# A fused two-layer kernel on one core: Pi's rows spread over a head's channels by DMA through DRAM in place of TensorE, and the products with Pi a tile later

## The chip, the cores and the metric

The kernel runs on one core of a Trainium2 chip, in one launch, in fp32 throughout. The metric is the device time in microseconds (us), the median over several executions. Engines are named as in the profile: PE is TensorE (PEld its weight loads), DVE is VectorE, ACT is ScalarE, POOL is GpSimd, SP is the engine that issues most DMA transfers.

## What is computed

Two layers over x of shape (2, 768, 64, 64): a state-space block (layer 0), then an attention without a score matrix (layer 1). Each layer takes a group norm of its input and adds its result to it. The change lies in layer 1, for which the reference is, with HEADS = 12, d = 64 channels per head and N = 4096 positions:

```python
w = (x3 @ W_qkv.T).reshape(B, N, HEADS, d).transpose(0, 2, 1, 3)
norm = jnp.sqrt(jnp.sum(w * w, axis=2, keepdims=True))
w_normed = w / jnp.maximum(norm, 1e-12)
logits = jnp.sum(w_normed ** 2, axis=-1) * temp
Pi = jax.nn.softmax(logits, axis=1)                      # over the 12 heads
Pi_n = Pi / (jnp.sum(Pi, axis=-1, keepdims=True) + 1e-08)
dots = jnp.einsum('bhn,bhnd->bhd', Pi_n, w ** 2)[:, :, None, :]
attn = 1.0 / (1.0 + dots)
out = -(w * Pi[..., None]) * attn                        # then @ W_out.T
```

So Pi has one value per head and position, and each is used for all 64 channels of its head.

## The kernel before

**Layout.** Channels lie on the 128 partitions, in KM = 6 chunks of 128 (two heads each), and positions along the free axis, in NQ = 8 tiles of QL = 512 positions per image. A matrix product of one chunk of outputs by one tile takes six 128x512 matmuls over the six input chunks; each fp32 matmul shows as two records in the trace.

**Order of the work.** Everything is issued in program order, written out by hand, each engine in its own in-order queue. Layer 0 runs to about 2780 us. Then, for image 0, the qkv products run in a block form with fewer multiplications (`strassen`), then `attention(0, ...)`, then a second `strassen` run (W_out for image 0, qkv for image 1), then `attention(1, ...)`, then W_out for image 1. Twelve ordinary products are kept back for each attention stage, so that TensorE has work while the softmax goes through the other engines. In the stage of image 0 they are qkv products of image 1, evicted by ScalarE (`p1_evict`, lines 677 and 678); in that of image 1 they are W_out products of image 0, evicted by VectorE with the residual addition (`p3_evict`, line 707) and stored. `half_a` issues three of a product's six matmuls (and the loads for the product three ahead), `half_b` the other three, then what it is handed, then the eviction.

**One tile of attention**, in the order of the steps:

- `squares`: ScalarE squares the six chunks of w (line 984), two tiles ahead.
- `head_rows`: TensorE sums the squares per head with weights `gcol` into `pr` (line 1006); ScalarE copies it to `lt` (line 1009).
- `head_columns`: four matmuls turn the 12 head rows into columns, `pl` (line 1017), positions on the partitions.
- `softmax_a`: VectorE takes the maximum `mx` (line 1023) and subtracts it (line 1025), ScalarE takes the exponential (line 1026).
- `softmax_b`: VectorE sums, takes the reciprocal and multiplies (lines 1032 to 1034), writes the result four times side by side into `pi` with padding (line 1036) and adds up `ph` (line 1037); TensorE transposes `pi` into `pt` (line 1041), ScalarE copies it to `pit` (line 1045).
- `spread`: for each chunk one matmul with the 0/1 weights `esel` repeats the two head rows of `pit` over 64 partitions each, into PSUM tiles `ppz` and `ppo` (line 1057).
- `times_pi`: VectorE multiplies w by the spread Pi (line 1063).
- `pi_sums`: VectorE multiplies that by w again and sums it up into `dots` (line 1070, with an accumulator read after it).

The loop over tiles j in `attention` overlaps the row and column steps and the softmax of tile j + 1 with the spread, products and sums of tile j. After the loop come one product, the sum of Pi over all positions `pp` (line 1107), `at` = -1/(1 + dots) on VectorE (lines 1112 to 1119), `behind()`, which issues the first loads of the next `strassen` run and scales its first tile by `at` (line 824), and one more product.

Of the kernel before, what the change touches and what calls it, by code (L numbers as in the profile page):

```python
# [7 lines left out]
F32 = mybir.dt.float32  # L8
# [6 lines left out]
P = 128  # L15
# [51 lines left out]
@with_exitstack  # L67
def both_layers(
    ctx, tc, nc, consts, x, in_wP, xp_wP, dt_wP, out_wT, pc_in, comb_in, pick_in, xsum_in, gavg_in, gsel_in, wo_dr, bc_dr, s_dr, x1, stats1,
    qkvP, woutP, temp_c, hcol_in, hsel_in, esel_in, out  # L70
):
    ident, ones, eps_c = consts

# [552 lines left out]
    ss = [gp.tile([P, KM, 2 * NQ], F32, name=f"ss{b}") for b in range(NB)]  # L626
    for t in ss:
        nc.gpsimd.memset(t, 0.0)
    x1s, w1s, pis, pits, ats, dots, phs = {}, {}, {}, {}, {}, {}, {}

    def gn_next(b):
        mv = gp.tile([P, KM, 2], F32, name=f"mv1_{b}")
# [126 lines left out]
    def product(n=1):  # L759
        for _ in range(n):  # L760
            half_a()
            half_b()
# [238 lines left out]
    def head_rows(b, j):  # L1001
        pr = psX.tile([P, 512], F32, tag="px", name=f"pr{b}_{j}")
        for m in range(KM):
            w2 = sqs.pop((b, j, m))
            r = 32 * (m % 4)
            nc.tensor.matmul(pr[r : r + 32, :], gcol[:, m, :], w2, start=(m < 4), stop=(m in (2, 3, 4, 5)))  # L1006
            give(w2)
        lt = wk.tile([P, QL], F32, tag="du", name=f"lt{b}_{j}", bufs=2)
        nc.scalar.copy(lt, pr)
        pits["lt"] = lt  # L1010

# [17 lines left out]
    def softmax_b(b, j):  # L1029
        e = pis.pop("e")  # L1030
        sm = small.tile([P, NB4], F32, tag="sm", name=f"sm{b}_{j}")
        nc.vector.tensor_reduce(sm, e, AX.X, ALU.add)
        nc.vector.reciprocal(sm, sm)
        nc.vector.tensor_mul(e, e, sm.unsqueeze(2).to_broadcast([P, NB4, HEADS]))
        pi = pi4[j % 2]
        nc.vector.tensor_copy(pi[:, :, :, :HEADS], e.unsqueeze(2).to_broadcast([P, NB4, 4, HEADS]))
        nc.vector.tensor_reduce(phs[b][:, j, :], e.rearrange("p q h -> p h q"), AX.X, ALU.add)

        pt = psS.tile([P, 512], F32, tag="st", name=f"pt{b}_{j}")
        for q in range(NB4):  # L1040
            nc.tensor.matmul(  # L1041
                pt[:, q * P : (q + 1) * P], pi[:, q, :, :].rearrange("p c h -> p (c h)"), ident, start=True, stop=True
            )
        pit = wk.tile([P, QL], F32, tag="delta", name=f"pit{b}_{j}", bufs=3)
        nc.scalar.copy(pit, pt)
        pits[b, j] = pit

    def spread(b, j, ms):

        for m in ms:  # L1050
            if m in (0, 4):
                pits["z"] = psZ.tile([P, 2, 512], F32, tag="pz", name=f"ppz{b}_{j}_{m}")
            if m == 2:
                pits["o"] = [psO.tile([P, 512], F32, tag=f"po{e}", name=f"ppo{e}_{b}_{j}") for e in range(2)]
            pb = pits["o"][m % 2] if m in (2, 3) else pits["z"][:, m % 2, :]
            r = 32 * (m % 4)
            nc.tensor.matmul(pb, esel[r : r + HEADS, m, :], pits[b, j][r : r + HEADS, :], start=True, stop=True)  # L1057
            pits[b, j, m] = pb

    def times_pi(b, j, ms):  # L1060
        for m in ms:
            w, v = w1s[b, m, j], take()
            nc.vector.tensor_mul(v, pits.pop((b, j, m)), w)
            w1s[b, m, j] = v
            pis[b, j, m] = w

    def pi_sums(b, j, ms):
        for m in ms:
            w = pis.pop((b, j, m))
            nc.vector.tensor_tensor_reduce(w, w1s[b, m, j], w, 1.0, 0.0, ALU.mult, ALU.add, dots[b][:, m, j : j + 1])  # L1070
            give(w)

    def attention(b, lead, more, behind):
        dots[b] = gp1.tile([P, KM, NQ], F32, name=f"dots{b}")
        phs[b] = gp1.tile([P, NQ, HEADS], F32, name=f"ph{b}")
        squares(b, 0)
        head_weights(b)
        product(lead)
        head_rows(b, 0)
        squares(b, 1)  # L1080
        half_a()
        head_columns(b, 0)
        softmax_a(b, 0)
        half_b(lambda: softmax_b(b, 0))
        for j in range(NQ):
            last = j + 1 == NQ
            if not last:
                head_rows(b, j + 1)
            spread(b, j, range(4))
            times_pi(b, j, range(4))  # L1090
            if j + 2 < NQ:
                squares(b, j + 2)
            half_a()
            if not last:
                head_columns(b, j + 1)
                softmax_a(b, j + 1)
            spread(b, j, (4, 5))
            pi_sums(b, j, range(2))
            half_b(lambda: last or softmax_b(b, j + 1))
            times_pi(b, j, (4, 5))  # L1100
            pi_sums(b, j, range(2, KM))

        ph = gp1.tile([P, HEADS], F32, name=f"phs{b}")
        nc.vector.tensor_reduce(ph, phs[b].rearrange("p j h -> p h j"), AX.X, ALU.add)
        product()
        pp = psS.tile([P, 512], F32, tag="st", name=f"pp{b}")
        nc.tensor.matmul(pp[:, :HEADS], ones, ph, start=True, stop=True)
        ppv = pp[:, :HEADS].rearrange("p (m e) -> p m e", e=2)
        rp = gp1.tile([P, KM], F32, name=f"rp{b}")
        for e in range(2):  # L1110
            h = slice(e * HD, (e + 1) * HD)
            nc.vector.tensor_scalar_add(rp[h, :], ppv[h, :, e], 1e-8)
        nc.vector.reciprocal(rp, rp)
        at = gp1.tile([P, KM], F32, name=f"at{b}")
        nc.vector.tensor_reduce(at, dots[b], AX.X, ALU.add)
        nc.vector.tensor_mul(at, at, rp)
        nc.vector.tensor_scalar_add(at, at, 1.0)
        nc.vector.reciprocal(at, at)
        nc.vector.tensor_scalar_mul(at, at, -1.0)
        ats[b] = at  # L1120
        behind()
        product(more)
# [7 lines left out]
    with tc.manual_schedule():  # L1130
# [236 lines left out]
        gcol = gp1.tile([P, KM, 32], F32, name="gcol")  # L1367
        hsel = gp1.tile([P, HEADS], F32, name="hsel")
        nc.sync.dma_start(hsel, hsel_in)
        esel = gp1.tile([P, KM, P], F32, name="esel")  # L1370
        nc.sync.dma_start(esel, esel_in)
        pi4 = [gp1.tile([P, NB4, 4, 32], F32, name=f"pi4_{j}") for j in range(2)]
        for pi in pi4:
            nc.gpsimd.memset(pi, 0.0)

        end = NQ0 + BEHIND + 2
# [46 lines left out]

@with_exitstack
def mamba_then_attention(
    ctx, tc, x, in_wP, xp_wP, dt_wP, out_wT, pc_in, comb_in, pick_in, xsum_in, qkvP, woutP, temp_c, ident_in, gavg_in, gsel_in, hcol_in, hsel_in, esel_in, out
):
    nc = tc.nc  # L1430
    keep = ctx.enter_context(tc.tile_pool(name="keep", bufs=1))
# [15 lines left out]
    bc_dr = [dram.tile([2 * NS, TL], F32, name=f"bc_dr{i}") for i in range(NI)]  # L1447

    s_dr = {k: dram.tile([KM // 2, 4, P, KM // 2, P], F32, name=f"s_dr_{k}") for k in ("p1", "p3")}
    both_layers(  # L1450
        tc, nc, consts, x, in_wP, xp_wP, dt_wP, out_wT, pc_in, comb_in, pick_in, xsum_in, gavg_in, gsel_in, wo_dr, bc_dr, s_dr, x1, stats1,
        qkvP, woutP, temp_c, hcol_in, hsel_in, esel_in, [out[b].rearrange("c h w -> c (h w)") for b in range(NB)],
    )


# [103 lines left out]
```

## Time and profile before

| What | Value |
|---|---|
| Time, median of 3 | 3739.17 us (3734.65 to 3747.25) |
| Profiled execution, its own time | 3740.45 us |
| Profiled execution, span of the trace | 3737.2 us |
| PE busy | 3540.6 us (95%) |
| DVE, ACT, POOL busy | 2870.0 (77%), 2565.7 (69%), 1775.4 (48%) us |
| Mean granted TensorE clock | 0.986 |
| Attention stage of image 0 | tiles from 2960.9 us, pp at 3062.1, next stage's first matmul at 3067.5 |
| Attention stage of image 1 | tiles from 3405.9 us, pp at 3508.9, next stage's first matmul at 3515.2 |
| Spread matmuls (line 1057) | 192 records, 587 to 692 ns each, overlapping |

The two attention stages take some 106 and 109 us, a seventeenth of the span together. The whole-span shares say little of them, so the stage is read from the trace by windows and timelines. In a timeline line the columns are the start and the length in us, the engine, the line of the kernel, the operation, result and operands, the shape, and in brackets the idle time before it with what ended it. In a windows line they are the stretch, its length, the busy time of PE, PEld, DVE, ACT and POOL with the number of instructions, the granted clock, the DMA share and GB/s. Consecutive matmul records overlap in the trace, so costs on TensorE are taken from start to start.

### The profile page before, as it was taken

To read this page: it belongs to the slowest core of one execution; us is meant where nothing else is said; L and a number is where in the kernel's file an instruction comes from. 1 tells how busy PE (TensorE), PEld (TensorE's weight loads), DVE (VectorE), ACT (ScalarE), POOL (GpSimd) and SP (SyncE) were. 2 spreads that over 40 slices of the span, in tenths; PEclk is the share of its full clock that TensorE was granted. 3 is DMA by queue.
4 is the path that set the end of the run, shared out by engine and by line. 5 is a ranking of instruction groups with operands and counts; after the bars stand their busy time and mean duration, and the time that the engine had idled before them with its cause. 6 is when DMAs were issued, how large, how long until landed. Compare 5 with 4: busy or idle time off the path is not lost. (4 is left out here: it accounts for less than half of the span.)

```text
span 3737.2 us, 37806 instructions
## 1 busy us (share of the span) xinstructions
PE 3540.6 (95%) x11098; PEld 1758.6 (47%) x11098; DVE 2870.0 (77%) x2614; ACT 2565.7 (69%) x4988; POOL 1775.4 (48%) x1809
## 2 busy tenths in 40 slices
PE   5877999999999999999899999999999999999999
PEld 3423333333333333333343333333346758886688
DVE  7699999999999999999999999997721362224522
ACT  2588888889888988888789888987733541244221
POOL 0245565565655655555555555554443313320232
PEclk9988999999999999999999999999999999999999
DMA  9677898889989899898889989897666628764487
GB/s 350 186 179 149 188 207 179 201 191 212 199 187 207 180 213 202 190 210 179 197 189 201 202 187 205 182 213 176 148 194 186 206 82 271 255 210 124 150 271 245
DMA packets 379724, 737.91 MB, mean 197 GB/s; under 512 B 44240, under 2 KB 116880, under 8 KB 375424
## 3 DMA queue, kind: packets, MB, share of 16 engines
q0 software_dynamic: 145632, 269.03, 42.3%
q1 hardware_dynamic: 233888, 466.49, 37.9%
q8 instruction: 89, 1.46, 0.2%
q14 instruction: 115, 0.94, 0.1%
HBM read 440.96 MB, written 60.03 MB: 134 GB/s over the span
## 5 line engine op out<-in xcount | busy, mean ns | idle before, releaser
L578 PE MATMUL po<-u,w 128*128 128x512 f32 x2256 | 1022.4, 603 | 50.2 <-DVE u L590 50.0
L352 PE MATMUL pa<-u,w 128*128 128x512 f32 (+1 forms) x2304 | 1039.0, 601 | 26.9 <-ACT carry L367 20.8
L514 DVE TENSOR_TENSOR_SCAN s<-da,s 128x2052 f32<-128x2052 f32 x192 | 851.1, 4433 | 19.2 <-DVE s L512 0.5
L352 PEld LDWEIGHTS pa<-u,w 128*128 128x128 f32 x2304 | 431.3, 192 | 620.2 <-issue 479.9
L578 PEld LDWEIGHTS po<-u,w 128*128 128x128 f32 x2256 | 421.3, 191 | 640.7 <-issue 541.5
L501 POOL TENSOR_TENSOR ysum<-da 128x1024 f32<-128x1024 f32 x192 | 384.7, 2003 | 588.5 <-DVE da L521 482.0
L436 DVE SCALAR_TENSOR_TENSOR acc<-xs,pc,acc 128x512 f32<-128x512 f32 x741 | 558.2, 753 | 44.6 <-PE acc L422 18.2
L489 ACT ACTIVATE da<-dl,neg_a 128x512 f32<-128x512 f32 x768 | 489.6, 713 | 0.0
L512 DVE TENSOR_TENSOR s<-du,bc 128x2048 f32<-128x2048 f32 x192 | 438.8, 2286 | 54.8 <-POOL du L493 54.3
L408 POOL DMA_DIRECT2D tm<-tm x309 | 267.6, 866 | 434.1 <-ACT tm L402 402.7
L521 DVE TENSOR_TENSOR da<-s,bc 128x2048 f32<-128x2048 f32 x192 | 440.0, 2292 | 6.3
L508 POOL DMA_DIRECT2D u<-ysum x384 | 378.6, 1249 | 3.3 <-issue 2.2
L390 ACT ACTIVATE acc<-xs,pc 128x512 f32<-128x512 f32 x192 | 132.4, 689 | 280.9 <-DVE u L436 279.7
L402 ACT ACTIVATE tm<-xs,pc 128x512 f32<-128x512 f32 x486 | 317.0, 717 | 4.7 <-DMA tm<-tm 3.6
L493 POOL TENSOR_TENSOR du<-dl,u 128x512 f32<-128x512 f32 x192 | 243.6, 1269 | 0.0
L414 POOL DMA_DIRECT2D u<-tm x177 | 203.0, 1147 | 62.3 <-issue 45.5
L861 PE MATMUL po_p<-v,w 128*128 128x256 f32 x672 | 172.5, 381 | 1.4 <-ACT po_p L958 1.4
L861 PE MATMUL po_p<-u,w 128*128 128x256 f32 x624 | 160.5, 381 | 0.0
L436 DVE SCALAR_TENSOR_TENSOR u<-xs,pc,acc 128x512 f32<-128x512 f32 x192 | 143.6, 748 | 9.8 <-PE pa L352 0.7
L806 POOL TENSOR_TENSOR v<-u 128x256 f32<-128x256 f32 x21 | 15.7, 758 | 278.2 <-ACT u L824 264.5
L861 PE MATMUL acc_p<-u,w 128*128 128x256 f32 x556 | 142.4, 380 | 3.7 <-DMA w<-woutP 2.5
L861 PE MATMUL psa_p<-u,w 128*128 128x256 f32 x554 | 141.0, 380 | 3.0 <-DMA w<-qkvP 2.3
(284 smaller groups left out, 4928.3 us busy)
## 6 DMA issues: line engine op xcount, KB each, us to landing
u<-ysum POOLq DMA_DIRECT2D x384, 256.0 KB, 5.8
tm<-tm POOLq DMA_DIRECT2D x309, 256.0 KB, 4.3
w<-in_wP SPq DMA_DIRECT2D x192, 384.0 KB, 4.8
w<-wo_dr SPq DMA_DIRECT2D x192, 384.0 KB, 5.2
u<-x SPq DMA_DIRECT2D x263, 256.0 KB, 5.4
w<-s_dr_p SPq DMA_DIRECT2D x288, 192.0 KB, 3.7
u<-tm POOLq DMA_DIRECT2D x177, 256.0 KB, 5.8
bc<-bc_dr SPq DMA_DIRECT2D x32, 1024.0 KB, 7.0
```

What stands on the lines that cost most here:

```text
L352: nc.tensor.matmul(pa[:, :nn], w[:, k, :], xts[i, k][:, :nn], start=(k == 0), stop=(k == KM - 1))
L402: nc.scalar.activation(tm.rearrange("p (h w) -> p h w", w=W), xs[:, dy : dy + TR, dx : dx + W], AF.Copy, scale=pc[:, c, PC_W + j : PC_W + ...
L408: nc.gpsimd.dma_start(tms[a][0], tms[a][q], accum_op=ALU.add)
L436: nc.vector.scalar_tensor_tensor(dst, xs[:, dy : dy + TR, dx : dx + W], pc[:, c, PC_W + j : PC_W + j + 1], acc, ALU.mult, ALU.add)
L489: nc.scalar.activation(das[g % 2][:, n, 1:], deltas[g], AF.Exp, scale=neg_a[:, c, n : n + 1])
L501: nc.gpsimd.tensor_add(ysum[:, 0 : 2 + g % 2 : 1 + g % 2, :], da[:, 0:2, 1:], da[:, 2:4, 1:])
L508: nc.gpsimd.dma_start(us[g], ysums(g, n), accum_op=ALU.add)
L512: nc.vector.tensor_mul(s[:, :, 1:], dus.pop(g).unsqueeze(1).to_broadcast([P, NS, TL]), bc[:, :NS, :])
L514: nc.vector.tensor_tensor_scan(sf, das[g % 2].rearrange("p n l -> p (n l)"), sf, 0.0, ALU.mult, ALU.add)
L521: nc.vector.tensor_mul(das[g % 2][:, :, 1:], s[:, :, 1:], bc[:, NS:, :])
L578: nc.tensor.matmul(po[e], w[:, kk, e * P : (e + 1) * P], us[i * KI + k], start=(k == 0), stop=(k == KI - 1))
L861: nc.tensor.matmul(dst, half[:, k, :], tiles[blocks[seq[i][0]][:3]][what][k], start=(start and k == 0), stop=(k == KH - 1), skip_group_che ...
```

## The change

The spread matmuls go. The transposes take the normalised softmax result `e` directly (12 columns) in place of the padded fourfold copy `pi`, which goes too, with its memsets and the weights `esel`. The 12 rows of `pit` are stored to a DRAM tile `pi_dr` of their own for each tile of positions. `load_pi` reads each head's row back from DRAM and broadcasts it to 64 partitions: 12 transfers per tile, into six SBUF tiles `pib` that are used again for every tile. `times_pi` reads `pib`. In the loop, the products with Pi and the Pi sums of tile j - 1 stand where those of tile j stood, and `load_pi` of tile j stands after them; the first four products and the last two keep their places around `half_a` and `softmax_a`. The last tile's products and sums follow the loop, between the halves of a product that stood as `product()` before pp.

```diff
@@ softmax_b
-        pi = pi4[j % 2]
-        nc.vector.tensor_copy(pi[:, :, :, :HEADS], e.unsqueeze(2).to_broadcast([P, NB4, 4, HEADS]))
         nc.vector.tensor_reduce(phs[b][:, j, :], e.rearrange("p q h -> p h q"), AX.X, ALU.add)
 
         pt = psS.tile([P, 512], F32, tag="st", name=f"pt{b}_{j}")
         for q in range(NB4):
-            nc.tensor.matmul(
-                pt[:, q * P : (q + 1) * P], pi[:, q, :, :].rearrange("p c h -> p (c h)"), ident, start=True, stop=True
-            )
-        pit = wk.tile([P, QL], F32, tag="delta", name=f"pit{b}_{j}", bufs=3)
-        nc.scalar.copy(pit, pt)
-        pits[b, j] = pit
-
-    def spread(b, j, ms):
+            nc.tensor.matmul(pt[:HEADS, q * P : (q + 1) * P], e[:, q, :], ident, start=True, stop=True)
+        pit = wk.tile([P, QL], F32, tag="du", name=f"pit{b}_{j}")
+        nc.scalar.copy(pit[:HEADS, :], pt[:HEADS, :])
+        nc.sync.dma_start(pi_dr[b][j], pit[:HEADS, :])
+
+    def load_pi(b, j, ms):
 
         for m in ms:
-            if m in (0, 4):
-                pits["z"] = psZ.tile([P, 2, 512], F32, tag="pz", name=f"ppz{b}_{j}_{m}")
-            if m == 2:
-                pits["o"] = [psO.tile([P, 512], F32, tag=f"po{e}", name=f"ppo{e}_{b}_{j}") for e in range(2)]
-            pb = pits["o"][m % 2] if m in (2, 3) else pits["z"][:, m % 2, :]
-            r = 32 * (m % 4)
-            nc.tensor.matmul(pb, esel[r : r + HEADS, m, :], pits[b, j][r : r + HEADS, :], start=True, stop=True)
-            pits[b, j, m] = pb
+            for e in range(2):
+                h = slice(e * HD, (e + 1) * HD)
+                nc.sync.dma_start(pib[m][h, :], pi_dr[b][j][2 * m + e : 2 * m + e + 1, :].partition_broadcast(HD))
 
     def times_pi(b, j, ms):
         for m in ms:
             w, v = w1s[b, m, j], take()
-            nc.vector.tensor_mul(v, pits.pop((b, j, m)), w)
+            nc.vector.tensor_mul(v, pib[m], w)
@@ attention
+        pib[:] = [wk.tile([P, QL], F32, tag=t, name=f"pi{t}{b}_{q}", bufs=3) for t in ("sq", "delta") for q in range(3)]
...
         half_b(lambda: softmax_b(b, 0))
+        load_pi(b, 0, range(KM))
+
         for j in range(NQ):
-            last = j + 1 == NQ
-            if not last:
+            if j + 1 < NQ:
                 head_rows(b, j + 1)
-            spread(b, j, range(4))
-            times_pi(b, j, range(4))
+            if j:
+                times_pi(b, j - 1, range(4))
             if j + 2 < NQ:
                 squares(b, j + 2)
             half_a()
-            if not last:
+            if j:
+                load_pi(b, j, range(4))
+            if j + 1 < NQ:
                 head_columns(b, j + 1)
                 softmax_a(b, j + 1)
-            spread(b, j, (4, 5))
-            pi_sums(b, j, range(2))
-            half_b(lambda: last or softmax_b(b, j + 1))
-            times_pi(b, j, (4, 5))
-            pi_sums(b, j, range(2, KM))
+            if j:
+                times_pi(b, j - 1, (4, 5))
+                load_pi(b, j, (4, 5))
+                pi_sums(b, j - 1, range(2))
+            half_b(lambda: j + 1 == NQ or softmax_b(b, j + 1))
+            if j:
+                pi_sums(b, j - 1, range(2, KM))
+        half_a()
+        times_pi(b, NQ - 1, range(KM))
+        pi_sums(b, NQ - 1, range(KM))
+        half_b()
 
         ph = gp1.tile([P, HEADS], F32, name=f"phs{b}")
         nc.vector.tensor_reduce(ph, phs[b].rearrange("p j h -> p h j"), AX.X, ALU.add)
-        product()
```

The rest of the diff removes `esel` and `pi4`, passes `pi_dr` through the calls, and drops `bufs=2` from `lt`.

More of the change, by code (lines that the diff above doesn't have):

```diff
@@ L69, in both_layers @@
     ctx, tc, nc, consts, x, in_wP, xp_wP, dt_wP, out_wT, pc_in, comb_in, pick_in, xsum_in, gavg_in, gsel_in, wo_dr, bc_dr, s_dr, x1, stats1,
-    qkvP, woutP, temp_c, hcol_in, hsel_in, esel_in, out
+    qkvP, woutP, temp_c, hcol_in, hsel_in, pi_dr, out
 ):
@@ L628, in both_layers @@
         nc.gpsimd.memset(t, 0.0)
-    x1s, w1s, pis, pits, ats, dots, phs = {}, {}, {}, {}, {}, {}, {}
+    x1s, w1s, pis, pits, ats, dots, phs, pib = {}, {}, {}, {}, {}, {}, {}, []
     def gn_next(b):
@@ L1007, in head_rows @@
             give(w2)
-        lt = wk.tile([P, QL], F32, tag="du", name=f"lt{b}_{j}", bufs=2)
+        lt = wk.tile([P, QL], F32, tag="du", name=f"lt{b}_{j}")
         nc.scalar.copy(lt, pr)
@@ L1369, in both_layers @@
         nc.sync.dma_start(hsel, hsel_in)
[L1370 to L1374, printed above, removed]
         end = NQ0 + BEHIND + 2
@@ L1427, in mamba_then_attention @@
 def mamba_then_attention(
-    ctx, tc, x, in_wP, xp_wP, dt_wP, out_wT, pc_in, comb_in, pick_in, xsum_in, qkvP, woutP, temp_c, ident_in, gavg_in, gsel_in, hcol_in, hsel_in, esel_in, out
+    ctx, tc, x, in_wP, xp_wP, dt_wP, out_wT, pc_in, comb_in, pick_in, xsum_in, qkvP, woutP, temp_c, ident_in, gavg_in, gsel_in, hcol_in, hsel_in, out
 ):
@@ L1449, in mamba_then_attention @@
     s_dr = {k: dram.tile([KM // 2, 4, P, KM // 2, P], F32, name=f"s_dr_{k}") for k in ("p1", "p3")}
+    pi_dr = [[dram.tile([HEADS, QL], F32, name=f"pi_dr{b}_{j}") for j in range(NQ)] for b in range(NB)]
     both_layers(
         tc, nc, consts, x, in_wP, xp_wP, dt_wP, out_wT, pc_in, comb_in, pick_in, xsum_in, gavg_in, gsel_in, wo_dr, bc_dr, s_dr, x1, stats1,
-        qkvP, woutP, temp_c, hcol_in, hsel_in, esel_in, [out[b].rearrange("c h w -> c (h w)") for b in range(NB)],
+        qkvP, woutP, temp_c, hcol_in, hsel_in, pi_dr, [out[b].rearrange("c h w -> c (h w)") for b in range(NB)],
     )
@@ L1503 @@
     hsel[32 * (hd // 2 % 4) + hd, hd] = 1.0
-    esel = np.zeros((P, DM), np.float32)
-    for r in range(0, P, 32):
-        esel[r + ch // HD, ch] = 1.0
     def by_chunk(w):
@@ L1545 @@
         "hsel_in": hsel,
-        "esel_in": esel.reshape(P, KM, P),
     }
```

## The prediction

> **What bounds the kernel now.** I first split the span with the windows view, to see which engine fills the attention stage: tiles of image 0 from 2960 to about 3062 us, of image 1 from 3406 to about 3509 us. Columns: length, busy time of PE, PEld, DVE, ACT, POOL, granted clock, DMA share, GB/s.
>
> ```profile
> 2990.00:3005.00 15.00, 15.00 (x75) 7.14 (x75) 12.40 (x37) 7.29 (x16) 0.00 (x0) 1.00 0.20 63
> 3400.00:3500.00 100.00, 98.82 (x434) 45.49 (x432) 72.52 (x205) 35.08 (x72) 0.00 (x0) 0.98 0.27 86
> ```
>
> TensorE never rests, VectorE has 12.4 of 15, GpSimd is idle, DMA is at 0.2 to 0.3. So TensorE sets the pace, and VectorE is not far behind. Then the timeline of TensorE over one tile (start, length):
>
> ```profile
> 2995.52 2.84 PE L667 MATMUL mmp<-v,w 128*128 128x512 f32 x6
> 2998.20 0.96 PE L1017 MATMUL pl<-hsel,lt 128*128 128x12 f32 x8
> 2999.09 1.13 PE L1057 MATMUL ppz<-pit,esel 12*128 12x512 f32 x4
> 3000.14 1.12 PE L667 MATMUL mmp<-v,w 128*128 128x512 f32 x2
> ...
> 3002.82 1.05 PE L1041 MATMUL pt<-ident,pi 128*128 128x128 f32 x8
> 3003.81 0.62 PE L1006 MATMUL pr<-v,gcol 128*32 128x512 f32 x1
> ...
> 3005.65 0.70 PE L1057 MATMUL ppz<-pit,esel 12*128 12x512 f32 x2
> ...
> 3006.72 2.84 PE L667 MATMUL mmp<-v,w 128*128 128x512 f32 x6
> ```
>
> Start to start: half a product 2.68, pl 0.89, two spreads 1.05, half a product 2.68, pt 0.99, pr 1.84, four spreads 1.07; sum 11.20 us, the tile's period, with no gap. Third, VectorE over the same tile, for the path pl, softmax, pt:
>
> ```profile
> 2999.20 0.21 DVE L1023 TENSOR_REDUCE mx<-pl 128x4 f32<-128x48 f32 x1 [1.09 <-PE pl L1017]
> 2999.44 0.21 DVE L1025 TENSOR_TENSOR e<-pl,mx 128x48 f32<-128x48 f32 x1
> 2999.56 0.68 DVE L1070 CUSTOM_DVE_ANT_0 u<-u,u 128x512 f32<-128x512 f32 x1
> ...
> 3001.23 0.21 DVE L1034 TENSOR_TENSOR e<-e,sm 128x48 f32<-128x48 f32 x1
> 3001.47 0.26 DVE L1036 COPY pi<-e 128x192 f32<-128x192 f32 x1
> ```
>
> VectorE waits for pl; 2.24 us later the normalised `e` is there, although two Pi sums stand in between, and pi is ready at 3001.73, 1.1 us before pt (3002.82). That slack is what the change spends. Fourth, the end of the stage:
>
> ```profile
> 3047.62 1.05 PE L1041 MATMUL pt<-ident,pi 128*128 128x128 f32 x8
> 3062.08 0.29 PE L1107 MATMUL pp<-phs,ones 128*128 128x12 f32 x2
> 3062.41 0.34 DVE L1112 TENSOR_SCALAR rp<-pp 64x6 f32<-64x6 f32 x2 [4.07 <-PE pp L1107]
> ```
>
> VectorE finished 4 us ahead of pp, under the product that stood before it.
>
> **Part by part.** *Spreads removed.* 1.05 + 1.07 = 2.12 us of TensorE per tile, all on the path: 16 tiles give at most 34 us. What is late next decides how much of it stays.
>
> *Products with Pi a tile later.* In a middle tile (j = 1 to 6) VectorE's order between pl and pt becomes mx, sub, two products with Pi, two Pi sums, sm, reciprocal, multiply. The products (L1063) follow each other every 0.60 us; the chain from mx to the end of the multiply grows from 2.24 to 2.24 + 2 x 0.60 = 3.44 us. TensorE has only half a product (2.68) to put there, not 2.68 + 1.05. So pt waits: mx begins 1.00 us after pl begins, pt 1.00 + 3.44 + 0.05 = 4.5 us after pl; TensorE is done with pl and half a product after 3.57. Idle 0.9 us. Behind pt in TensorE's queue stand pr of the next tile, the half product and the next pl, for which VectorE waits: a loop through both engines. Its period: 1.00 + 3.44 + 0.05 + pt 1.09 (2969.12 to 2970.21, where pt waited too) + pr 1.84 + half 2.68 = 10.1 us. VectorE's own sum is smaller: 3.44 + 0.2 (ph) + 4 x 0.61 + 4 x 0.60 = 8.5, with the residual addition of image 1 (0.6) 9.1. So a middle tile gains 1.1, not 2.1. Tile 0 has no products in that path (mx to multiply took 2.4 us at 2966.4, with a table load in it): TensorE binds and it gains 2.1. Per image 2.1 + 6 x 1.1 = 8.7 us.
>
> The products read Pi from SBUF and no longer from PSUM. The Trainium skill (VectorE: DVE Perf Modes, "The TRN2 errata") charges 58 cycles for an SBUF source and 120 for PSUM, which would be 0.065 us less per product, 0.13 in the loop, 1.6 us over 12 tiles. The nearest rows: 128x2048 from SBUF 2.286 us (L512), 128x512 from PSUM 0.681 (L1063). Both are about 0.15 over one element per 0.96 GHz cycle, so I take no gain, and keep 0 to -1.6 us.
>
> *The end of an image.* Before, the last products hid under three products. Now VectorE still owes, from the end of the multiply of tile 7: ph 0.2, four sums of tile 5 2.45, products and sums of tile 6 3.6 + 3.7, of tile 7 3.6 + 3.7, total 0.3: 17.5 us. pp waits for all of it. TensorE has pt and two products, 1.1 + 10.7 = 11.8, then idles about 5.8 us; after pp one product, 5.4. From pt to the first matmul of the next stage: 17.5 + 5.4 = 22.9, against 19.8 before (3047.62 to 3067.45): 3.1 lost. Image 1 adds three residual additions (1.8): 24.7 plus some 0.3 of weight wait, against 22.9 (3492.27 to 3515.16): 2.1 lost.
>
> *The clock.* These rows show what idling can cost here:
>
> ```profile
> 3494.50 0.70 PE L1057 MATMUL ppz<-pit,esel 12*128 12x512 f32 x2 [1.18 <-DVE u L1063]
> 3496.25:3499.67 3.42, 3.42 (x6) 1.00 (x4) 3.42 (x7) 0.00 (x0) 0.00 (x0) 0.55 0.00 0
> ```
>
> After a gap of only 1.18 us beside 12-row matmuls the clock went to half for 3.4 us, 1.7 us lost. A gap of 1.40 us at 2854 between dense matmuls brought no drop. The Trainium skill (TensorE: Matmul & The Clock Gate, "Why this matters for your kernels") says only gaps over about 3 us count. By the rule the 0.9 us gaps cost nothing. By the row some could: a stretch of 3.4 us holding the gap, a 12-column pt and part of pr is about as thin as the one that dropped. Laid against the drops of this trace, I estimate none or one per image. I take none in the tiles and keep one each, 3.4 us, for the range. The 5.8 us gap at pp drops the clock by rule and row alike: the product after it runs at half speed for some 3 us, 1.5 lost per image.
>
> *pt.* Still eight records of 128 columns, spaced 0.107 us, with fewer weight columns: 0, at most -0.1 per tile. pi's copy (0.2 us) leaves VectorE; counted in the chain. The 384 KB load and two memsets before the stage: 0.
>
> *DMA, SP.* Per tile one store (24 KB) and 12 loads of 128 KB, all on SP, beside 2 or 3 that stand there. Unhindered, SP issues every 0.47 us (3528.36, 3528.82, 3529.30): 15.5 x 0.47 = 7.3 of 10.1 us. No 128 KB row is in this stage; from below hcol (96 KB) landed in 2.0, from above 384 KB of weights in 3.2 here: I take 2.6. After pt: copy 0.6, store landed at about 2.7, loads 0 to 3 issued by 6.5, landed by 9.1; VectorE wants the fourth at 13.4. Hidden by 4 us. Queued behind SP's wait for the store are weights needed three products later. Traffic: 768 packets of 0.097 us (37.9% of 16 engines, 233888 packets) over 16 engines, 4.7 us per tile, beside 2 to 3: it fits. If the cover is gone: first rival.
>
> **Sum.** 3740.45 (profiled execution: span 3737.2 and 3.25 around it) - 2 x 8.7 + 3.1 + 2.1 + 2 x 1.5 = 3731.2. The profiled run is 1.3 above the median 3739.17; against that -8.0 us, -0.21%. I treat 0.3%, 11.2 us, as what a measurement can tell from no change.
>
> **Rivals.** *A: the loop through softmax binds, as summed*, chance 0.50, own range 3726 to 3737: late clock drops up, shorter products down; a quarter of it lies under 3728.
>
> *B: TensorE or VectorE alone binds* because the chain is shorter than I add up. Tiles then take 9.1 us: 2.1 x 7 = 14.7 per image, 12 more in all: 3719. For: VectorE has the time, 9.1 at most. Against: in-order VectorE. Chance 0.28.
>
> *C: SP and the transfers bind; slower.* In the changed kernel's instruction list each SP transfer also waits for the one eight before it. Pace is then landing/8:
>
> ```profile
> bc<-bc_dr SPq DMA_DIRECT2D x32, 1024.0 KB, 7.0
> ```
>
> This broadcast, as many bytes as eight of the new loads, takes 7.0 us in a busy stage. At 7.0 each load: 0.875 x 15.5 = 13.6 us per tile, 2.4 more than now; 14 tiles, 34 us, less 4 (first tiles), plus 8 (ends and clock): 3778. It turns the result slower by 0.3% once a tile takes 11.8, a landing of 6.1 us. Against: DMA at 0.2. Chance 0.16.
>
> *D: nothing comes of it*: clock drops eat the gain: five in the twelve middle tiles give 5 x 1.7 = 8.5 back, about 3740. Chance 0.06.
>
> **Numbers.** Under 3728: a quarter of A and B, 0.40. Over 3750: C, 0.16. Between: 0.44. The range runs from B's 3719 to 3745, past D and leaving out most of C.
>
> **What would show it.** Right: middle tiles 10.1 us pr to pr, VectorE named as releaser of about 0.9 us before pt, a gap of 5 to 7 us at pp with half clock after it, loads landing under 4 us. Wrong: products that wait for DMA (C), tiles of 9.1 with no gap before pt (B), half clock inside the tiles (D).

## The result, and the profile after

| | Before | After |
|---|---|---|
| Time, median of all runs | 3741.06 us | 3749.64 us |
| Ratio | 1 | 1.0023 (95% interval 1.0014 to 1.0031) |
| Profiled execution, its own time | 3740.45 us | 3757.72 us |
| Stage of image 0, first pr matmul to the next stage's first matmul | 106.6 us | 111.2 us |
| Stage of image 1 | 109.3 us | 113.7 us |
| Both stages | 215.9 us | 224.9 us |

The change costs 8.6 us, where 8 to 9 us of gain were predicted. The two stages alone account for it: +9.0 us. (The profiled execution after is 8 us above its median, and most of that surplus lies ahead of the stages: that of image 0 starts 7 us later.) Stage and tile lengths here are counted from the trace, from the start of a tile's first pr matmul to that of the next. The windows view over the two stages, with the columns as above, first of the kernel before:

```profile
2960.86:3067.45 106.59, 105.80 (x455) 48.66 (x455) 71.00 (x209) 53.83 (x112) 2.73 (x4) 1.00 0.21 62
3405.88:3515.16 109.28, 107.39 (x455) 49.00 (x455) 78.45 (x221) 36.97 (x72) 2.89 (x5) 0.98 0.27 86
```

and of the changed kernel:

```profile
2967.93:3079.13 111.20, 92.97 (x360) 44.31 (x360) 70.06 (x201) 53.52 (x112) 5.58 (x9) 0.92 0.56 175
3419.47:3533.17 113.70, 93.82 (x359) 44.38 (x359) 76.77 (x212) 36.88 (x72) 5.34 (x8) 0.91 0.66 200
```

TensorE, idle for 0.8 and 1.9 us of its stages before, is now idle for 18 to 20 us of each, and its clock is down to 0.92 and 0.91, from 1.00 and 0.98. The DMA share has more than doubled. So the work left TensorE, and the time did not. By tiles:

| us | tile 0 | tile 1 | tiles 2 to 5 | pt of tile 7 to pp | pp to next stage |
|---|---|---|---|---|---|
| image 0 before | 11.20 | 11.20 | 11.20 each | 14.46 | 5.37 |
| image 0 predicted | 9.1 | 10.1 | 10.1 each | 17.5 | 6.9 |
| image 0 after | 8.93 | 14.52 | 9.86 each | 21.84 | 8.48 |
| image 1 before | 11.20 | 11.20 | 11.20 each | 16.65 | 6.25 |
| image 1 after | 8.93 | 10.36 | 13.45, 10.60, 11.04, 11.51 | 21.58 | 8.33 |

(Turn j of the loop begins with pr of tile j + 1; the last that ends with another pr is tile 5.) The middle tiles of image 0 are as predicted. The timelines of TensorE and of VectorE there:

```profile
3019.20 0.94 PE L1039 MATMUL pt<-ident,e 128*12 128x128 f32 x7 [0.86 <-DVE e L1034]
```

```profile
3015.71 0.21 DVE L1023 TENSOR_REDUCE mx<-pl 128x4 f32<-128x48 f32 x1 [1.30 <-PE pl L1017]
3016.07 1.28 DVE L1054 TENSOR_TENSOR u<-pidelta,u 128x512 f32<-128x512 f32 x2
...
3018.94 0.21 DVE L1034 TENSOR_TENSOR e<-e,sm 128x48 f32<-128x48 f32 x1
```

From mx to the end of the multiply 3.44 us (3.44 predicted), then pt after 0.86 us of idling (0.9 predicted). Three places are not as predicted. First, the second tile of image 0. SP, ScalarE and TensorE there:

```profile
2979.82 3.79 SPq L1049 DMA_DIRECT2D pisq<-pi_dr  x6
2983.66 3.79 SPq L1049 DMA_DIRECT2D pidelta<-pi_dr  x6
2987.55 0.53 SPq L661 DMA_DIRECT2D w<-qkvP  x1
2988.12 0.43 SPq L652 DMA_DIRECT2D u<-x  x1
```

```profile
2992.79 0.81 ACT L655 ACTIVATE u<-u,bias,scale 128x512 f32<-128x512 f32 x1 [5.05 <-DMA u<-x]
2993.51 0.56 ACT L1009 COPY lt<-pr 128x512 f32<-128x512 f32 x1
```

```profile
2994.13 1.27 PE L1017 MATMUL pl<-hsel,lt 128*128 128x12 f32 x8 [3.63 <-ACT lt L1009]
```

A load of x for a kept-back product stands behind tile 0's 12 loads on SP, which take 7.7 us. ScalarE's norm of that x waits 5.05 us for it, the copy `lt` stands behind the norm, and pl behind `lt`. Second, the ends. VectorE and TensorE at the end of image 0:

```profile
3061.70 0.69 DVE L1054 TENSOR_TENSOR v<-pisq,v 128x512 f32<-128x512 f32 x1 [0.66 <-DMA pisq<-pi_dr]
3062.98 0.69 DVE L1054 TENSOR_TENSOR u<-pidelta,v 128x512 f32<-128x512 f32 x1 [0.58 <-DMA pidelta<-pi_dr]
3064.53 0.69 DVE L1054 TENSOR_TENSOR u<-pidelta,v 128x512 f32<-128x512 f32 x1 [0.85 <-DMA pidelta<-pi_dr]
```

```profile
3070.62 0.57 PE L1107 MATMUL pp<-phs,ones 128*128 128x12 f32 x2 [10.30 <-DVE phs L1105]
```

The products with Pi wait for their loads one by one, in tiles 6 and 7 some 3.6 us together, and TensorE idles 10.3 us ahead of pp, where 5.8 was predicted (10.04 us in image 1). Third, image 1, where no middle tile reaches 9.86. There SP sets the pace (start, and time that SP is held):

```profile
3478.20 3.65 SPq L1049 DMA_DIRECT2D pisq<-pi_dr  x6
3481.95 3.73 SPq L1049 DMA_DIRECT2D pidelta<-pi_dr  x6
3485.78 0.50 SPq L1042 DMA_DIRECT2D pi_dr<-pit  x1
3486.38 0.35 SPq L688 DMA_DIRECT2D out<-u  x1
3486.79 0.41 SPq L684 DMA_DIRECT2D v<-x  x1
3487.29 0.40 SPq L661 DMA_DIRECT2D w<-woutP  x1
3488.69 3.65 SPq L1049 DMA_DIRECT2D pisq<-pi_dr  x6
```

SP is never free but for 1.0 us, from 3487.69 to 3488.69. In that it waits for the landing of the Pi store that it issued itself. Its waits in the stage of image 1 show that, and a second kind (in total, times and longest):

```profile
SPq L1049 <- DMA pi_dr<-pit: 9.3, 8, 3.3
SPq L1049 <- DMA w<-woutP: 2.2, 4, 0.9
```

The second is a load of Pi that waits for the transfer eight before it, a load of weights, to land. One turn of SP takes 7.5 (loads) + 2.0 (store, out, x, w with the gaps) + 1.0 (the wait) = 10.5 us, more than the 9.86 that TensorE and VectorE need.

The longest tile, of 13.45 us, shows one way in which a full SP reaches TensorE. SP, ScalarE, VectorE and TensorE there:

```profile
3453.25 0.37 SPq L688 DMA_DIRECT2D out<-v  x1
```

```profile
3456.14 0.63 ACT L984 ACTIVATE v<-u 128x512 f32<-128x512 f32 x1 [5.32 <-DMA out<-v]
```

```profile
3459.01 0.20 DVE L1032 TENSOR_REDUCE sm<-e 128x4 f32<-128x48 f32 x1 [1.80 <-ACT e L1026]
```

```profile
3459.72 1.67 PE L1039 MATMUL pt<-ident,e 128*12 128x128 f32 x7 [3.86 <-DVE e L1034]
```

The tile that this store of `out` sends was ready at 3447.68 (line 707), but on SP the store stands behind 12 loads and the store of Pi. ScalarE's next square needs the buffer that the store frees and waits 5.32 us for it; the exponential stands behind the squares, the softmax and pt behind the exponential. In the stage of image 1 ScalarE waits 10.1 us for such stores; in the kernel before it waits for none.

So the theory tested below, S: a load of Pi holds SP longer than I costed, about 0.6 us and not 0.47, SP is full, and what stands behind the loads comes late. The rival L (T in some expectations): it is the bytes and their landing that the products wait for. O in the expectations is a third one: VectorE's new order alone loses the time. The profile's list of issues has the median landing in its last column:

```profile
pisq<-pi_dr SPq DMA_DIRECT2D x96, 128.0 KB, 3.2
```

### The profile page after: what moved, and what is told of

The parts are those of the page before. It is cut to its first block, busy times and chain, and to the rows that moved or that the text cites. A ratio compares the mean times of both kernels' runs of the same rounds, so it can differ in the third digit from the quotient of the medians.

```text
span 3755.9 us, 37795 instructions
## 1 busy us (share of the span) xinstructions
PE 3517.9 (94%) x10906; PEld 1752.6 (47%) x10906; DVE 2867.7 (76%) x2598; ACT 2564.7 (68%) x4988; POOL 1775.0 (47%) x1807
## 5 line engine op out<-in xcount | busy, mean ns | idle before, releaser
L352 PE MATMUL pa<-u,w 128*128 128x512 f32 (+1 forms) x2304 | 1039.7, 601 | 29.5 <-ACT carry L367 19.9
L436 DVE SCALAR_TENSOR_TENSOR acc<-xs,pc,acc 128x512 f32<-128x512 f32 x741 | 558.2, 753 | 46.3 <-PE acc L422 19.9
L861 PE MATMUL po_p<-v,w 128*128 128x256 f32 x708 | 181.6, 380 | 1.4 <-ACT po_p L958 1.4
L861 PE MATMUL po_p<-u,w 128*128 128x256 f32 x588 | 152.8, 379 | 0.0
L861 PEld LDWEIGHTS po_p<-v,w 128*128 128x128 f32 x708 | 134.6, 190 | 20.5 <-ACT po_p L958 1.8
L505 ACT ACTIVATE u<-u,pc 128x512 f32<-128x512 f32 x192 | 136.8, 712 | 2.1 <-POOL du L493 2.1
L861 PE MATMUL psa_p<-u,w 128*128 128x256 f32 x486 | 127.2, 380 | 4.9 <-DMA w<-qkvP 4.8
```

Source lines behind the costliest of these rows:

```text
L352: nc.tensor.matmul(pa[:, :nn], w[:, k, :], xts[i, k][:, :nn], start=(k == 0), stop=(k == KM - 1))
L436: nc.vector.scalar_tensor_tensor(dst, xs[:, dy : dy + TR, dx : dx + W], pc[:, c, PC_W + j : PC_W + j + 1], acc, ALU.mult, ALU.add)
L861: nc.tensor.matmul(dst, half[:, k, :], tiles[blocks[seq[i][0]][:3]][what][k], start=(start and k == 0), stop=(k == KH - 1), skip_group_che ...
```

## The experiments

All ratios are to the kernel before on the same chip. The stage sums come from each kernel's profiled execution, so that a difference of a few microseconds between a stage sum and a median is no finding.

| Kernel | Ratio (95%) | Both stages, us | Ends (pt to pp), us |
|---|---|---|---|
| before | 1 | 215.9 | 14.5, 16.7 |
| after | 1.0023 (1.0014 to 1.0031) | 224.9 | 21.8, 21.6 |
| no_dma | 0.9976 (0.9968 to 0.9985) | 205.0 | 17.6, 19.7 |
| late | 1.0024 (1.0018 to 1.0030) | 224.3 | 20.6, 23.8 |
| tiny | 0.9991 (0.9983 to 0.9999) | 213.6 | 17.6, 19.4 |
| split | 0.9987 (0.9980 to 0.9993) | 209.3 | 19.5, 19.4 |
| group | 1.0025 (1.0017 to 1.0033) | 221.2 | 23.2, 23.3 |
| act_store | 1.0015 (1.0007 to 1.0023) | 220.5 | 18.8, 22.1 |
| x_first | 1.0010 (1.0001 to 1.0019) | 218.5 | 22.6, 22.1 |
| soft_first | 1.0005 (0.9998 to 1.0013) | 212.9 | 20.4, 24.8 |
| lanes | 0.9978 (0.9971 to 0.9984) | 206.1 | 17.6, 19.4 |
| lanes12 | 0.9990 (0.9982 to 0.9998) | 209.0 | 17.6, 19.8 |
| best | 0.9970 (0.9959 to 0.9982) | 202.9 | 20.9, 21.8 |
| best_act | 0.9972 (0.9962 to 0.9982) | 202.9 | 22.5, 21.8 |
| pool_all | 0.9986 (0.9976 to 0.9996) | 210.0 | 24.9, 22.9 |
| pair | 1.1067 (1.1052 to 1.1083) | 612.9 | 72.3, 71.9 |
| pair_soft | 1.1028 (1.1013 to 1.1043) | 599.0 | 80.1, 82.4 |
| pair16 | 1.0030 (1.0019 to 1.0040) | 226.2 | 20.2, 20.8 |
| pair16_soft | 0.9982 (0.9975 to 0.9989) | 207.9 | 20.3, 22.8 |

**no_dma: no store and no loads of Pi.**

```diff
-        nc.sync.dma_start(pi_dr[b][j], pit[:HEADS, :])
...
-                nc.sync.dma_start(pib[m][h, :], pi_dr[b][j][...])
+        for t in pib:
+            nc.gpsimd.memset(t, 0.08)
```

> The changed kernel without its stores of Pi and without its loads; pib is filled with a constant once per image, so the products with Pi are made with that constant. Theory S (SP: 12 broadcast loads at 0.62 us of SP each, 7.4 us, plus a store and three more transfers fill SP's time per tile, so loads, weights and x tiles come late): without them the middle tiles are 9.9 us in both images, the gap before pp falls from 10 to about 6 us, stages about 102 and 104 us in place of 111.1 and 113.7; whole kernel 3731 us, ratio to before 0.9975. Rival O (VectorE's new order alone loses the time, the transfers are hidden): stages stay within 2 us of 111 and 114, ratio 1.002. Rival T (the transfers are slow in themselves, whoever issues them) says the same as S here.

3731.38 us, the time predicted for the whole change (3731.2). All middle tiles of both images take 9.86 us, the ends 17.6 and 19.7. What VectorE's order and the ends cost was sized rightly, then; the transfers take back 19.9 us of the stages.

**late: the products and sums a tile later alone, with TensorE's spread.** The kernel before, with `spread`, `times_pi` and `pi_sums` of tile j - 1 where those of tile j stood, and the last tile's after the loop.

> The kernel before with spread, products and sums of tile j - 1 where those of tile j stood, and the last tile's after the loop between the halves of a product, as in the change; Pi is still spread by TensorE and nothing goes through DRAM. It prices the later products alone. Theory: TensorE still binds the middle tiles at 11.2 us (the longer path through VectorE, 3.44 us, has the two spreads and half a product, 3.7 us, beside it); tile 0 gains 2.1; the end costs 3 to 4 us and the half clock after its gap 1.5 to 3; each stage 2 to 5 us longer than the 106.6 and 109.3 of before, ratio 1.001 to 1.0025. Rival (the order costs nothing, all of the loss is in the transfers): ratio 1.000.

3751.51 us. The middle tiles stay at 11.20 us, tile 0 of each image gains 2.2 (8.97), the ends grow by 6.1 and 7.2 us, where 3 to 4 were expected. So the delay alone costs 8.4 us of the stages; going on to no_dma, without the spreads, then gives 224.3 - 205.0 = 19.3 us; the transfers cost 19.9. The parts of the change, taken in this order: +8.4, -19.3, +19.9, together +9.0. (In late the last two products stay behind the softmax, and mx to the multiply still takes 2.24 us, not the 3.44 of its expectation; so the price of VectorE's longer path lies in the second part.)

**tiny and split: fewer bytes, or two queues.** In tiny, from tile 1 on, each of the 12 loads carries 16 of the 512 positions (the rest of each Pi tile is stale). In split GpSimd issues every second load.

```diff
-                nc.sync.dma_start(pib[m][h, :], ...)
+                (nc.sync, nc.gpsimd)[e].dma_start(pib[m][h, :], ...)
```

> The changed kernel in which, from tile 1 of each image on, each of the 12 loads moves only 16 positions per row, 64 bytes for each of 64 partitions; the rest of pib keeps tile 0's values, so Pi is not the right one there. Same number of transfers, same waits, 1/32 of the bytes. Theory S with a price per transfer: SP still needs about 0.6 us for each, stages within 2 us of the changed kernel's 111 and 114, ratio 1.002. Theory S with a price that comes from the bytes in flight, and rival T: the loads cost SP 0.35 us or less, and stages fall to about 105 and 105 (tile 0's full loads still stand in front of the x tile in image 0), ratio 0.998. Rival O: no change, 1.002.

> The changed kernel with the loads of each chunk's second head issued by GpSimd, which is idle in this stage, and the first head's by SP. Theory S: SP's time per tile falls from 9.4 to 5.7 us, waits for loads and late x tiles go, middle tiles 9.9 us in both images, stages about 103 and 105, ratio 0.998. Rival T: the same bytes land as late as before, stages 110 to 114, ratio 1.002. Rival O: no change. GpSimd's own cost, 1.0 to 1.2 us for each transfer by its rows of before, is 6 to 7 us of a 9.9 us tile, and fits.

tiny 3738.24 us, split 3735.75 us. In tiny a load of 64 bytes per partition holds SP for 0.587 us in the median, as one of 2 KB does: SP's price is one per transfer. But the 1/32 of bytes did take away 11.3 us of the stages, where S with a price per transfer expected no more than 2 per stage, so the bytes are not innocent: the store lands sooner, and SP waits for that less (4.0 us in the stage of image 1 and not 9.3). What stays in tiny is the tile of 14.8 us in image 0, behind tile 0's full loads, and 10.2, 12.7 and 10.9 us in tiles of image 1. split keeps the bytes and the shape of the loads and takes 15.6 us away; in image 1 all its middle tiles take 9.86. This speaks for S, with L as a part.

**group: 4 chunks in one transfer.** One transfer of 512 KB brings a head of each of chunks 0 to 3, into one tile for the four chunks; with chunks 4 and 5 as before there are 6 transfers per tile.

> The changed kernel with the four rows of chunks 0 to 3 of one parity loaded by one transfer of 512 KB, so six transfers per tile in place of 12 and the same bytes. Theory S with a price per transfer: SP falls to 6 x 0.62 + 2 = 5.7 us per tile; stages about 103 to 106, ratio 0.998 to 0.999. With a price by bytes: a 512 KB transfer holds SP four times as long, SP stays at 9 us per tile and the stages within 2 us of 111 and 114. Rival T: as the latter. Rival O: no change, 1.002.

3750.99 us, no better than the changed kernel: a miss for S in its plain form. SP is held for 0.61 us by each large transfer too, and six of them would leave it time; but VectorE's products now wait 12.5 and 9.3 us in the two stages for the 512 KB to land (4.8 and 3.5 us for all loads of the changed kernel), and the profile has these loads in its chain of work that ended last. The ends take 23.2 and 23.3 us. Fewer transfers do not help if each product waits longer for its own.

**act_store, x_first, soft_first: one reordering each.** ScalarE issues the store; tile 0's loads stand behind the loads of the next product; the softmax of the next tile stands ahead of two products and two sums.

```diff
-        nc.sync.dma_start(pi_dr[b][j], pit[:HEADS, :])
+        nc.scalar.dma_start(pi_dr[b][j], pit[:HEADS, :])
```

> The changed kernel with the store of Pi issued by ScalarE right behind its copy pit, and no longer by SP; nothing else. In the changed kernel the store waits in SP behind the loads of the tile before, and the next loads wait in SP for its landing. Theory S (SP's time per tile: 12 loads at 0.63 us, 2.1 us for the other transfers and 0.8 us of waiting for the store make 10.4 us, more than the 9.86 us of the other engines): SP falls to 7.6 + 1.5 = 9.0 us, image 1's middle tiles go to 9.9 us, its stage from 113.7 to about 105; image 0's end from 21.8 to about 18.5, its stage from 111 to about 108, tile 1 (14.5 us) staying; ratio about 0.999. Rival T (landing of the bytes): no more than 2 us gained in each image, ratio 1.002. Rival O: the same, 1.002.

> The changed kernel with the 12 loads of tile 0 issued after the weight and x transfers of the first product of the loop and no longer ahead of them. Theory Q (image 0's tile 1, 14.5 us, is the x tile that stood in SP behind those loads: ScalarE's norm waited for it, and the copy lt stood behind the norm): tile 1 falls to 9.9 us, image 0's stage from 111 to about 105 (4.7 us of tile, of which 1.8 is half clock, 1 less at the end); image 1's stage stays at 111 to 114; ratio about 1.000. Rival (tile 1 is late because tile 0's Pi itself arrives late): tile 1 stays above 13 us, ratio 1.002.

> The changed kernel with softmax_b's steps ahead of the last two products with Pi and the first two sums, and their loads behind it; VectorE's path from pl to pt is then as short as in tile 0. Rival O (VectorE's order costs 0.9 us per tile, transfers are hidden): 12 middle tiles give 0.9 each, ratio about 0.999. Theory S (SP needs 10.4 us per tile whatever VectorE's order): tiles do not get shorter than 10 us on average, the wait moves from before pt to before the products, ratio 1.001 to 1.003.

act_store 3748.59 us, not to be told from the changed kernel, where S expected a ratio of about 0.999: the loads still wait for the store to land, and the second tile of image 0 even takes 16.0 us. x_first 3747.22 us: the second tile falls from 14.52 to 9.92 us, which shows the cause of that tile; of those 4.6 us, 1.5 are lost again later in image 0, in tile 6 and the end, since SP's lag is only met later. soft_first 3744.51 us. S expected its tiles not to get under 10 us on average, and was wrong there: they fall to 8.93 us in image 0, with no wait before pt. But SP's loads come every 9.4 us:

```profile
3023.74 3.64 SPq L1049 DMA_DIRECT2D pisq<-pi_dr  x6
3033.12 3.64 SPq L1049 DMA_DIRECT2D pisq<-pi_dr  x6
```

SP falls behind TensorE tile by tile, and the ends of 20.4 and 24.8 us give part of it back. Its stages lie 2.9 us under before while its median lies 2 us above, with an interval that includes no change.

**lanes and lanes12: the same bytes, other shapes.** In both, one row of a chunk is repeated over all 128 partitions, so that the second head of each chunk gets the first head's Pi. lanes does it with one transfer per chunk (6 per tile), lanes12 with two of 256 positions (12 per tile, as in the changed kernel).

```diff
-            for e in range(2):
-                h = slice(e * HD, (e + 1) * HD)
-                nc.sync.dma_start(pib[m][h, :], pi_dr[b][j][2 * m + e : 2 * m + e + 1, :].partition_broadcast(HD))
+            for e in range(2):
+                c = slice(e * QL // 2, (e + 1) * QL // 2)
+                nc.sync.dma_start(pib[m][:, c], pi_dr[b][j][2 * m : 2 * m + 1, c].partition_broadcast(P))
```

> As the changed kernel, but each chunk's Pi tile is filled by one transfer that repeats one row over all 128 partitions, in place of two of 64 (the second head of each chunk gets the first head's Pi: the output is not the reference's). The same bytes are written into SBUF, by 6 transfers per tile and not 12. Theory S (each broadcast load costs SP some 0.6 us whatever it carries, and SP with 12 of them, a store, the product's transfers and a wait takes over 9.9 us per tile): SP's loads fall to some 3.7 us per tile, all middle tiles of both images take 9.9 us, the second tile of image 0 some 10 to 12, the ends 19 to 20 us; 3734 to 3738 us, ratio to the kernel before 0.998 to 0.999. If the loads cost SP twice as much each when they fill twice the partitions (1.2 us), nothing changes: about 3750 us. Rival L (the bytes and their landing hold it, as the kernel with 512 KB transfers suggests): about 3750 us, ratio 1.002 to 1.003.

> As the kernel that repeats one row of each chunk over 128 partitions (so again the second head gets the first head's Pi, and the output is not the reference's), but with each load cut into two of 256 positions: 12 transfers per tile as in the changed kernel, the same bytes as there, each into 128 partitions. Theory P (the target's 64 partitions make the price): 0.32 us each on SP, some 0.45 us from start to start, 5.5 us per tile, 2 us less than the changed kernel; all middle tiles 9.9 us, the second tile of image 0 some 12 to 13 us; 3735 to 3740 us, ratio 0.9985 to 0.9995. Rival N (the number of transfers makes it): 0.55 us and more each, 3745 to 3750 us, as the changed kernel.

lanes 3734.11 us, lanes12 3738.00 us. With every byte of the changed kernel (DMA share 0.60 and 0.69 in the stages of lanes) the loss is gone but for 1.1 us of the stages in lanes and 4.0 in lanes12, against no_dma. SP in lanes12, at a middle tile of image 1:

```profile
3471.61 2.69 SPq L1049 DMA_DIRECT2D pisq<-pi_dr  x6
3474.43 3.20 SPq L1049 DMA_DIRECT2D pidelta<-pi_dr  x6
3478.53 0.31 SPq L1042 DMA_DIRECT2D pi_dr<-pit  x1
```

A load that repeats one row over 128 partitions holds SP for 0.32 us alone and 0.42 in a burst, where one over 64 holds it for 0.45 alone and 0.59 in a burst; from start to start in a burst 0.47 against 0.64 us, counted from the traces. That is 12 x 0.17 = 2.0 us per tile, and those 2 us are what SP lacked: lanes12 takes 15.9 of the 19.9 us away, at the same count and bytes. ScalarE's waits for the stores of `out` in image 1 fall from 10.1 to 6.0 us with it. L falls as the main cause (the loads of lanes12 even land later, 3.6 and 3.7 us in the median), and so does the count; what decides is the shape of the transfer and the time for which that holds SP. The Trainium skill (DMA: Bandwidth & Descriptors, "Rules for kernel authors") advises one 128-partition transfer in place of two to disjoint halves, since both halves spread over the same DMA engines. In lanes that held, but not by way of the DMA engines: what ran out was SP's time to issue. In pair and pair16 below, one transfer per chunk did not help.

**best, best_act, pool_all: what the loads' owner is worth, with the right output.** best joins split, x_first and soft_first; best_act adds act_store; pool_all is soft_first with all loads on GpSimd.

> As the changed kernel, with three moves together: the loads of the second head of each chunk are issued by GpSimd, tile 0's loads stand behind the transfers of the first product of the loop, and the softmax of the next tile stands ahead of the last two products with Pi and of the first two sums on VectorE. Theory S: the three take away different losses (SP's 7.6 us of loads per tile halved, the second tile's 14.5 us back to 9, the 0.9 us wait of the transposes for VectorE), so they add up but for the end of a stage, where VectorE's work of two tiles stays: tiles of 8.9 us in image 0 and 9 to 9.5 in image 1, ends of 20 to 22 us, stages together 200 to 205 us against 215.9 before; 3727 us (3723 to 3732), ratio 0.996. If VectorE is the bound by then, what the loop gains comes back at the end, and it lies where the kernel with only the split lies, at 3736 us.

> As the kernel with the three moves, with the store of Pi issued by ScalarE, which has just made its source, and not by SP. Theory S: SP's wait for the source of the store goes, the wait of the loads for the store's landing stays; 0 to 2 us less than with the three moves, about 3726 us. If ScalarE's issue stands in the way of its evictions and squares: 1 to 3 us more than with the three moves.

> As the changed kernel, with all 12 loads of a tile issued by GpSimd (which has nothing else to do in these stages) and the softmax of the next tile ahead of the last two products and the first two sums. Nothing stands before the loads of x and of the weights on SP any more. Theory S: GpSimd needs 12 x 0.52 = 6.2 us per tile for the issue, less than a tile, and nobody waits behind it; tiles of 8.9 us, no 14.5 us tile, ends of 20 to 23 us; 3725 to 3731 us. Rival L (landing of the loads): the products wait for the loads as in the changed kernel; 3738 to 3745 us.

best 3729.37 us, 0.30% under the kernel before, the fastest of this study; best_act 3731.22 us is not to be told from it. The stages of best:

```profile
2968.57:3067.87 99.30, 89.91 (x359) 43.28 (x359) 69.87 (x201) 53.41 (x112) 29.51 (x56) 0.95 0.67 195
3411.57:3515.17 103.60, 90.11 (x359) 43.28 (x359) 76.30 (x212) 36.98 (x72) 29.31 (x55) 0.95 0.82 219
```

The tiles of image 0 take 8.93 us, TensorE's own sum, those of image 1 9.5 and once 10.3. Of GpSimd's 29 us here 25 are the issue of 48 loads per image, 0.52 us each, and nothing waits behind them. The ends stay at 21 to 22 us: VectorE owes two tiles there. pool_all 3733.56 us, over its range: one queue of 12 x 0.52 us is enough for tiles of 8.93 us in image 0, but image 1 has a tile of 12.1, and the ends take 24.9 and 22.9.

**pair, pair_soft, pair16, pair16_soft: the cheap shape with the right output.** pair loads both rows of a chunk in one transfer, two rows times 64 repeats. pair16 stores each row eight times, and loads 16 rows times 8 repeats. The _soft kernels add soft_first and x_first.

```diff
+            rows = pi_dr[b][j][2 * m : 2 * m + 2, :]
+            nc.sync.dma_start(pib[m], rows.unsqueeze(1).to_broadcast([2, HD, QL]))
```

> As the changed kernel, but the two rows of a chunk are loaded by one transfer: each row is repeated over 64 partitions, 128 in all. The output is the reference's. 6 transfers per tile and not 12, the same bytes. Theory P (a transfer into 64 partitions holds SP for 0.59 us, one into 128 for 0.32 us, and that alone was the loss): SP's loads take 0.32 us each as in the kernel that repeated one row, the stages are those of that kernel, 102 to 103 and 103 to 104 us; 3734 us, ratio 0.9975 to 0.9985. Rival Q (one source row in place of two is what made that kernel's transfers cheap): 0.5 us and more each, the second tile of image 0 over 12 us, stages 105 us and more; 3738 to 3745 us.

> As the kernel with one transfer per chunk, with the softmax of the next tile ahead of the last two products with Pi and the first two sums, and tile 0's loads behind the transfers of the first product of the loop. Theory P: SP has time to spare, so TensorE's own 8.9 us per tile is reached in image 0 and 9.0 to 9.5 in image 1, where VectorE's products, sums and evictions take as long; ends of 19 to 21 us, as VectorE's work stays two tiles behind; stages together 197 to 203 us against 215.9 before; 3726 us (3722 to 3731), ratio 0.996. If the end gives back what the tiles gain, 3733 us, as with one transfer per chunk alone.

> As the changed kernel, but Pi is stored with each head's row written eight times one after the other, and a chunk's tile is loaded by one transfer that reads its 16 rows and repeats each over 8 partitions, 128 in all. The output is the reference's. Theory K (the source's first dimension of 2 held each whole load of the kernel with one transfer per chunk to two of the 16 DMA engines, 5.2 us each; with 16 it goes over all of them): SP busy 0.3 to 0.4 us per load, 6 per tile, nothing waits in the loop; the store of eight times the bytes lands somewhat later (3 to 4 us and not 2.8), which only the end of a stage could see; stages 102 to 106 us each, 3734 to 3739 us, ratio 0.998 to 0.9995. Rival Q (two rows or repeats in the middle of a transfer are slow as such): the loads take 2 us and more each, over 3760 us.

> The kernel with one transfer per chunk from 16 stored rows, with the softmax of the next tile ahead of the last two products with Pi and the first two sums, and tile 0's loads behind the transfers of the first product of the loop. Theory K with theory S: 8.9 us per tile in image 0, 9.0 to 9.5 in image 1 where VectorE is as long, ends of 19 to 22 us; stages together 197 to 204 us; 3726 us (3722 to 3731), ratio 0.995 to 0.997, level with or a little under the kernel with three moves. If the store's later landing or the end gives it back: 3732 to 3736 us.

pair 4144.74 us and pair_soft 4127.57 us: the largest misses here. SP, VectorE and the window of image 0 in pair:

```profile
3027.17 5.21 SPq L1048 DMA_DIRECT2D pidelta<-pi_dr  x1
```

```profile
3042.26 0.69 DVE L1053 TENSOR_TENSOR v<-pidelta,u 128x512 f32<-128x512 f32 x1 [5.14 <-DMA pidelta<-pi_dr]
```

```profile
2963.22:3269.42 306.20, 104.01 (x360) 48.57 (x360) 72.77 (x201) 54.07 (x112) 4.33 (x7) 0.66 0.19 63
```

In a row of such loads the later ones hold SP for some 5.2 us each, and six of them make tiles of 30 to 40 us, most of them 34 to 35, at a DMA share of only 0.19. The Trainium skill (same page and section) says that an outermost dimension of c under 16, such as the 2 rows here, confines the whole transfer to at most c of the 16 engines. The trace agrees. While one such load runs, the DMA share is 0.13, which is two engines of 16:

```profile
3027.20:3032.30 5.10, 2.18 (x6) 0.63 (x4) 0.69 (x1) 0.25 (x1) 0.00 (x0) 1.00 0.13 49
```

pair16, with 16 outermost, is out of that hole (0.55 us per load, 3751.47 us), so reading two rows is not what is slow. But it is no gain: its loads hold SP nearly as long as those into 64 partitions, though they fill 128, so it is not the number of partitions alone that makes a load cheap; and its store of eight times the bytes lands later (SP waits 23.7 us for it in image 0), so the second tile takes 17.4 us. Theory K was right on the two engines and wrong on the cheap price. pair16_soft 3735.47 us is faster than before, but over its range of 3722 to 3731 and not faster than best. The cheap load of lanes was not found with the right output.

## Why the prediction was wrong

- *Spreads removed, and the loop through softmax:* right. Middle tiles 9.86 us without the loads' trouble (10.1 predicted), tile 0 8.93 (9.1), idle 0.86 (0.9).
- *Products from SBUF:* right, no gain: 0.684 to 0.688 us against 0.679 to 0.683 from PSUM.
- *The end of an image:* right in itself. Without transfers 17.6 and 19.7 us, 17.5 and 19.3 predicted. In the changed kernel the loads add 4.2 and 1.9.
- *The clock:* half after each pp gap, as predicted; pp to the next stage takes 7.7 and 7.6 us without transfers (6.9 and 7.2 predicted) and 8.5 and 8.3 with them, since the half clock lasts 4.6 and 4.4 us after pp (no_dma) and not some 3. "None in the tiles" was wrong, as a consequence: where tiles wait for the transfers the clock is at 0.50 for 3.4 us each (windows from 2994.83, 3459.04 and 3482.94 us); no_dma has no half clock in its tiles.
- *DMA, SP:* this is the step that failed, in two of its terms. "Unhindered, SP issues every 0.47 us ... 15.5 x 0.47 = 7.3 of 10.1 us": the spacing came from transfers into 128 partitions. A load into 64 takes 0.64 from start to start, so the turn of SP is 9.5 us, and 10.5 with its wait for the store; the 2.8 us of spare time was -0.4. lanes12 takes this term away with one queue, 15.9 us of stages, and split with a second queue and the costly shape, 15.6. And "Queued behind SP's wait for the store are weights needed three products later" left out the loads of x, which are needed within the tile: 14.5 us in the second tile of image 0, which x_first takes away. It left out the stores of `out` too, whose buffers ScalarE needs: the tile of 13.45 us in image 1. No run moves these stores alone.
- "Hidden by 4 us" was true of one tile by itself; it had no account of a queue whose lag adds up over eight tiles and comes due at the end.

So the sum's terms for TensorE and VectorE gave 9.2 us of gain in the stages, 10.9 were there (no_dma), and the transfers, costed at nothing, took 19.9. Rival C named the right queue, with the wrong price: landings stayed at 3.2 us, half of its turning point of 6.1, its wait for the transfer eight before came to 2.2 us in the stage of image 1, and SP's own issue time was the bound. I had put 0.16 on it. The sign "loads landing under 4 us" came true in the median and told nothing, since landing is counted from the issue, and the time was lost before it.

## What to carry to other kernels

When work is moved to DMA, add up the issuing queue for one period with the price of that very shape of transfer, measured in a burst, and count its waits as occupancy; here that came to 9.5 of 9.9 us before the waits and 10.5 with them, a bound and not a cover. Ask for every transfer that the new ones are moved ahead of when it is needed next: a small load, and a store for the buffer that it frees. Work put off by one tile is not free even where the loop hides it: here the ends of the two stages grew by 6.2 us without any transfers (no_dma), and by 13.3 with the spreads still on TensorE (late).

## What had not been expected of the hardware

- A load that repeats one row over 64 partitions holds SP longer (0.59 us in a burst) than one that repeats it over 128 (0.42), whether it carries 64 B or 2 KB to each of the 64. A load of 16 rows times 8 repeats, also into 128, holds it for 0.55. Why is open.
- One transfer with two source rows outermost ran at 256 KB in 5.2 us and held SP for as long; with one row repeated over 128 partitions, the same bytes held it for 0.32 us.
- The store of 24 KB to DRAM made SP wait up to 3.3 us before the loads that read it, more than the issue of five of them.
